# Graph transformer, then graph attention: scores and both contexts of a pair stand together in TensorE's order

## The chip, the core and the metric

The kernel runs on one core of one Trainium2 chip. The core has five engines that run side by side, each through its own instructions in order: TensorE (PE, matrix products), VectorE (DVE), ScalarE (ACT), GpSimd (POOL) and SyncE (SP, which here issues the DMAs). They wait for one another through semaphores. The metric is the time on the device in microseconds (us), lower is better. All arithmetic is float32.

## The reference

There are 128 graphs of 128 nodes with 512 features. Two layers follow one another, both ahead of them a layer norm and a relu, both with the input added at the end:

```python
h = relu(layernorm(x))
q, k, v = h @ Wq.T + bq, h @ Wk.T + bk, h @ Wv.T + bv      # 8 heads of 64
scores = (q @ k.T) / 8 * (adj + adj)                       # for each head, 128 x 128
attn = softmax(scores, axis=-1)
x = x + (attn @ v) @ Wo.T + bo                             # the contexts of all heads, side by side

h = relu(layernorm(x))
Wh = h @ W
e = leaky_relu(Wh @ a[:512] + (Wh @ a[512:]).T, 0.2)
att = softmax(where(adj > 0.5, e, -9e15), axis=1)
x = x + elu(att @ Wh)
```

## The kernel before

Graphs are handled in pairs (64 of them). The projections to q, k and v are made for two pairs at a time, by a scheme with seven products of half-size blocks instead of eight. The work is cut into some 130 small steps. A list, ORDER, says in which order the steps of different pairs are recorded: `name:lag` records step `name` of pair p - lag. Every engine runs its part of that list in order, so the list is the schedule.

The steps of the first layer's attention, for one graph `b` (graphs a and b of a pair are 2p and 2p + 1; step names in the margin are followed by a or b in the list):

```python
ps1 = ctx.enter_context(tc.tile_pool(name="ps1", bufs=6, space=PSUM))   # six banks for all other products
ps2 = ctx.enter_context(tc.tile_pool(name="ps2", bufs=1, space=PSUM))   # one score buffer, two banks
work = ctx.enter_context(tc.tile_pool(name="work", bufs=1))
...
def scores(b):                                     # sca, scb
    sc = ps2.tile([P, H, S], F32, name="sc", tag="ps2")
    for j in range(C):
        for s in range(2):
            r = slice(s * D, (s + 1) * D)          # 64 of the 128 rows of the array
            nc.tensor.matmul(sc[:, s * C + j, :], qT[r, j, cols], kT[r, j, cols], start=True, stop=True)

def weigh(b):                                      # ata, atb: scores times the adjacency
    at = work.tile([P, H, S], F32, name="at")
    nc.vector.scalar_tensor_tensor(at, scs.pop(b), QSCALE, adj..., op0=OP.mult, op1=OP.mult)

def maxima(b):                                     # mxa, mxb
    nc.vector.tensor_reduce(nmx, at, AX.X, OP.max, negate=True)

def exps(b, k):                                    # exa0 .. exa3: two heads each, on ScalarE
def shares(b, k):                                  # rca0, rca1: reciprocals of the sums
def normalise(b, k):                               # nma0 .. nma3: two heads each, on ScalarE

def flip_blocks(b):                                # fla, flb: 32 x 32 blocks transposed
    at = ats.pop(b)[0]
    trs[b] = work.tile([P, S // Q, H, Q], F32, name="tr")
    nc.vector.transpose(trs[b], at.rearrange("p h (j k) -> p j h k", k=Q))

def send_blocks(b):                                # bla, blb: to memory, one DMA
    nc.sync.dma_start(blocks[b]..., trs.pop(b)...)

def place_blocks(b):                               # pla, plb: back, each block to its place, four DMAs
    d = blocks.pop(b)
    aTs[b] = work.tile([P, S // Q, H, Q], F32, name="aT")
    for j in range(S // Q):
        nc.sync.dma_start(aTs[b][j * Q : (j + 1) * Q]..., d[:, :, j, :]...)

def context(b):                                    # pca, pcb
    aT = aTs.pop(b)
    pc = ps1.tile([P, C, S], F32, name="pc", tag="ps1")
    for j in range(C):
        for s in range(2):                         # 64 of the 128 columns of the array
            head = 2 * j + s
            nc.tensor.matmul(pc[s * D : (s + 1) * D, j, :], v[..., head * D : (head + 1) * D], aT[:, :, s * C + j, :],
                             start=True, stop=True)

def keep_context(b):                               # pea, peb
    nc.scalar.copy(rows_of(cxT, b % 2), pcs.pop(b))
...
for p in range(early, N + late):
    for step, lag in ORDER:
        pair = p - lag
        for do in tables.get(pair, {}).get(step), first_use.get((pair, step)):
            if do:
                do()
```

The other steps that are named later: U1 to U11 are the products for q, k and v of a later group, F the first evictions of their sums (ScalarE), A the additions (VectorE); o0 to o6 are the output products of the first layer and od their additions to x; st, pw, nm and h2 are the second layer norm, d the dot products with `a`, pb, wm, pr, m1, e1 and sw the second attention; g0, g1 gather with it, w0 to w6 are its products with W, zc and wd the evictions of those, ez, fa and fb the elu and the last additions, so the store. fa and fb are 1024-wide VectorE passes, as are hd0 and hd1 (the hidden rows of a later pair) and sh (a constant row).

Of the kernel before, what the change touches and what calls it, by code (L numbers as in the profile page):

```python
# [8 lines left out]
F32 = mybir.dt.float32  # L9
# [4 lines left out]
P = 128  # L14
# [3 lines left out]
H = 8  # L18
D = 64
Q = 32  # L20
# [4 lines left out]
def kernel(  # L25
# [19 lines left out]
    B, S, E = x.shape  # L45
# [9 lines left out]
    work = ctx.enter_context(tc.tile_pool(name="work", bufs=1))  # L55
# [5 lines left out]
    xs, x0s, adjs, adjTs, hAs, hSs = {}, {}, {}, {}, {}, {}  # L61
# [93 lines left out]
    def token_sum(h, s, k):  # L155

        if k == 0:
            nc.vector.tensor_tensor(s[:, 0], h[:, 2], h[:, 3], OP.add)
        elif k == 1:
            nc.vector.tensor_tensor(s[:, 1], s[:, 0], h[:, 0], OP.subtract)  # L160
        elif k == 2:
            nc.vector.tensor_tensor(s[:, 2], h[:, 0], h[:, 2], OP.subtract)
        else:
            nc.vector.tensor_tensor(h[:, 2], h[:, 1], s[:, 1], OP.subtract)
# [16 lines left out]
    st0, rows0, qks, vs, scs, ats, trs, blocks, aTs, pcs = ({} for _ in range(10))  # L181
# [45 lines left out]
            nc.vector.scalar_tensor_tensor(h, h, 0.0, row, op0=OP.max, op1=OP.mult)  # L227

    def hidden_sum(g, k):
        if k == 0:  # L230
            hSs[g] = grp.tile([P, 3, 2, 2 * S], F32, name="hS")
        token_sum(hAs[g], hSs[g], k)

# [119 lines left out]

    def flip_blocks(b):
        at = ats.pop(b)[0]
        trs[b] = work.tile([P, S // Q, H, Q], F32, name="tr")
        nc.vector.transpose(trs[b], at.rearrange("p h (j k) -> p j h k", k=Q))  # L357

    def send_blocks(b):
# [2 lines left out]

    def place_blocks(b):
        d = blocks.pop(b)
        aTs[b] = work.tile([P, S // Q, H, Q], F32, name="aT")
        for j in range(S // Q):
            nc.sync.dma_start(
                aTs[b][j * Q : (j + 1) * Q].rearrange("k i h q -> k i (h q)"), d[:, :, j, :].rearrange("i k x -> k i x")
            )
# [152 lines left out]
    def spread_u():  # L522
# [13 lines left out]
    ORDER = [  # L536
        (step.split(":")[0], int(step.split(":")[1]))
        for step in """
        w5:4 o4:2 ata:0 U2:0 w6:4 mxa:0 sw:3 pca:1 od4:2 plb:1 g0:3 zc5:4 o5:2 od4c:2 wd6:4 o6:2 fa:4 exa2:0 hs1:1
        g1:3 exa0:0 ez:4 F2:0 U1:0 ge0:3 U8:1 fb:4 exa1:0 ge1:3 od5:2 od6:2 rca0:0 exa3:0 st0:2 st1:2 gs0:3 t0:0  # L540
        rca1:0 w0:3 nma1:0 U4:0 w1:3 gs2:3 scb:0 pw:2 pcb:1 so:4 A3:20 nm:2 pea:1 t1:0 nma0:0 gs1:3 nma2:0 nma3:0
        gs3:3 zc0:3 h21:2 A8:1 A9:1 fla:0 U11:1 atb:0 h20:2 hs3:1 F4:0 mxb:0 peb:1 F1:0 U3:0 d10:2 o0:1 A11:1 F3:0
        d11:2 A7:-37 A2:0 U5:0 cs0:1 exb0:0 A10:28 f0:0 cs1:1 lT:0 lt:2 exb1:0 F5:0 exb2:0 A4:21 exb3:0 U6:0 rcb0:0
        nmb0:0 F6:0 wd1:3 U7:0 A5:0 F8:-10 F7:0 o1:1 F11:10 cs2:1 l0:-1 d00:2 hd0:0 rcb1:0 s0:0 A1:19 nmb1:0 w2:3
        hd1:0 nmb3:0 zc2:3 pb:2 U9:0 F9:0 hs0:0 lx:1 o3:1 A6:0 d01:2 w4:3 nmb2:0 wm:2 sh:1 bla:0 od0:1 la:-1 pr:2
        U10:0 w3:3 od1:1 o2:1 F10:0 hs2:0 pla:0 flb:0 m1:2 zc4:3 od2:1 sca:-1 blb:0 cs3:1 e1:2 wd4c:3
        """.split()
    ]

    def steps(p):  # L550
# [3 lines left out]
        for s, n in (("a", a), ("b", b)):  # L554
            table |= {
                "sc" + s: lambda n=n: scores(n),
                "at" + s: lambda n=n: weigh(n),
                "mx" + s: lambda n=n: maxima(n),
                "fl" + s: lambda n=n: flip_blocks(n),
                "bl" + s: lambda n=n: send_blocks(n),  # L560
                "pl" + s: lambda n=n: place_blocks(n),
                "pc" + s: lambda n=n: context(n),
                "pe" + s: lambda n=n: keep_context(n),
            }
            for k in range(4):
                table[f"ex{s}{k}"] = lambda n=n, k=k: exps(n, k)
                table[f"nm{s}{k}"] = lambda n=n, k=k: normalise(n, k)
            for k in range(2):
                table[f"rc{s}{k}"] = lambda n=n, k=k: shares(n, k)
# [41 lines left out]
        if odd and (g + 2) * 2 < N:  # L611
            for k in range(4):
                table[f"hs{k}"] = lambda k=k: hidden_sum(g + 2, k)
# [11 lines left out]
    with tc.manual_schedule():  # L625
# [10 lines left out]
        for k in range(4):  # L636
            hidden_sum(0, k)
        for n, u in enumerate(SEQ):
            firsts, adds = product(0, u[0], int(u[1]))
            if n == 2:  # L640
                weight_sums(wq_sb)
            if n == 4:
                first_stats(2)
            if n == 6:
                hidden_T(2, rows[2], "h2")
            if n == 8:
                weight_sums(wk_sb)
            if n == 10:
                first_stats(3)
            if n == 12:  # L650
                hidden_T(3, rows[3], "z")
                load_x0(4)
            if n == 14:
                for k in range(4):
                    hidden_sum(1, k)
            firsts()
            adds()
# [59 lines left out]
```

## Time and profile before

| | before |
|---|---|
| time, median of 3 runs | 2436.83 us (2435.96 to 2436.95) |
| span of the profiled run | 2433.9 us |
| granted TensorE clock, mean | 0.996 of full speed |
| TensorE matmul busy | 2395.6 us |
| VectorE busy | 1993.2 us |
| ScalarE busy | 1449.3 us |
| busiest kinds of matmul | seven-product projections (acc), output and second-layer products (row_a, row_c), scores (sc, 148.7 us), contexts (pc, 140.1 us) |

The profile is one execution on the chip. In it a float32 matmul stands as two records. A line of a group reads: source line, engine, operation, tile written <- tiles read, shapes, number, then busy time and mean ns of one, then the idle time of its engine just before, with what ended most of it. In a matmul's line `64*128` or `128*64` are the rows and columns of the array in use. In a timeline the records of one kind that follow one another are merged: start, time from the first start to the last end, number. The durations of matmuls overlap, so the time a group takes on TensorE is read from its start to the start of the next.

### The profile page before, as it was taken

The numbers are of one execution on the slowest core, as the hardware profiler recorded it, in microseconds if no ns is written. First come the engines' busy times: TensorE is split into PE (matmuls) and PEld (weight loads), VectorE is DVE, ScalarE is ACT, GpSimd is POOL, SyncE is SP. The second block draws the span as 40 slices with busy tenths as digits, with TensorE's granted clock in tenths as the row PEclk, the third lists the DMA queues.
The fourth block names the chain that finished last, engine by engine and source line by source line (L and its number), as shares of the span: only waits on it lengthen the run. The fifth ranks groups of instructions, "written<-read, shape, count | busy, mean of one in ns | idle before, by whom it ended". The sixth has DMA issues, their size and how long they took to land.

```text
span 2433.9 us, 40532 instructions
## 1 busy us (share of the span) xinstructions
PE 2395.6 (98%) x14264; PEld 2055.1 (84%) x14264; DVE 1993.2 (82%) x3909; ACT 1449.3 (60%) x4811; POOL 180.3 (7%) x323
## 2 busy tenths in 40 slices
PE   8999999999999999999999999999999999999987
PEld 7788888888888888888888888888888888888876
DVE  5788888888888888888888888888888888887786
ACT  2566556656565665565665656655656655666573
POOL 1000000000000000000000000000000000000000
PEclk9999999999999999999999999999999999999998
DMA  4435434445343454344453434453444544443331
GB/s 156 122 110 147 129 115 119 137 135 139 113 132 109 142 140 143 101 135 121 135 148 111 133 109 138 135 145 99 139 118 135 148 118 125 116 140 116 104 112 65
DMA packets 255275, 306.09 MB, mean 126 GB/s; under 512 B 21856, under 2 KB 181600, under 8 KB 254432
## 3 DMA queue, kind: packets, MB, share of 16 engines
q1 hardware_dynamic: 251568, 303.37, 42.7%
q8 instruction: 112, 1.84, 0.3%
q14 instruction: 91, 0.75, 0.1%
q0 software_dynamic: 1920, 0.13, 0.1%
q10 hardware_dynamic: 1584, 0.01, 0.0%
HBM read 202.64 MB, written 100.79 MB: 125 GB/s over the span
## 4 chain that ended last, share of the span: by engine, by line
PE 96%; DVE 2%; ACT 1%; issue 0%; DMA 0%; POOL 0%; SPq 0%; POOLq 0%; DVEq 0%; ACTq 0%
PE acc_a L261 27%; PE row_a L302 23%; PE acc_c L261 14%; PE row_c L302 9%; PE acc_b L261 7%; PE sc L323 6%; PE pc L386 5%; PE pg L464 5%; PE pb L432 1%; DVE junk L423 0%; DVE nmx L336 0%; PE pt L202 0%; ACT at L341 0%; DVE st L172 0%; DMA x<-in_x 0%
## 5 line engine op out<-in xcount | busy, mean ns | idle before, releaser
L341 ACT ACTIVATE at<-at,nmx 128x128 f32<-128x128 f32 x1024 | 398.6, 394 | 90.7 <-DVE nmx L336 90.6
L302 PE MATMUL row_a<-w,gT 128*128 128x256 f32 x1280 | 338.5, 388 | 15.1 <-DVE z L482 14.2
L350 ACT ACTIVATE at<-at,rs 128x128 f32<-128x128 f32 x1024 | 331.8, 394 | 0.0
L302 PE MATMUL row_a<-wo,cxT 128*128 128x256 f32 x1280 | 328.8, 380 | 0.1
L302 PEld LDWEIGHTS row_a<-w,gT 128*128 128x128 f32 x1280 | 239.3, 191 | 55.6 <-issue 9.2
L478 ACT COPY z<-row_a 128x256 f32<-128x256 f32 x256 | 94.9, 371 | 301.0 <-PE row_a L302 298.6
L302 PEld LDWEIGHTS row_a<-wo,cxT 128*128 128x128 f32 x1280 | 237.8, 190 | 30.8 <-DVE x L400 0.7
L400 DVE TENSOR_TENSOR x<-row_a,x 128x256 f32<-128x256 f32 x320 | 134.9, 422 | 144.5 <-PE row_a L302 139.8
L329 DVE SCALAR_TENSOR_TENSOR at<-sc,adj 128x1024 f32<-128x1024 f32 x128 | 156.8, 1225 | 98.5 <-PE sc L323 97.3
L278 ACT ACTIVATE kT<-acc_a,bk 128x256 f32<-128x256 f32 x256 | 107.5, 471 | 178.4 <-PE acc_a L261 178.4
L176 POOL TENSOR_SCALAR mv<-mv 128x2 f32<-128x2 f32 x128 | 32.8, 256 | 2196.3 <-ACT at L341 1858.8
L341 ACT ACTIVATION_READ_ACCUMULATOR at<-at,nmx 128x1 f32 x1024 | 195.3, 191 | 0.0
L278 ACT ACTIVATE qT<-acc_a,bq 128x256 f32<-128x256 f32 x256 | 105.7, 463 | 123.6 <-PE acc_a L261 123.6
L172 DVE BATCH_NORM_STATS2 st<-x 128x6 f32<-128x512 f32 x256 | 172.6, 674 | 4.7 <-DMA x<-in_x 4.6
L357 DVE STREAM_TRANSPOSE tr<-at 128x1024 f32<-128x1024 f32 x128 | 158.1, 1235 | 8.4 <-ACT at L350 8.3
L323 PEld LDWEIGHTS sc<-kT,qT 64*128 64x128 f32 x2048 | 124.2, 187 | 42.5 <-issue 42.1
L336 DVE TENSOR_REDUCE nmx<-at 128x8 f32<-128x1024 f32 x128 | 155.9, 1218 | 3.3
L323 PE MATMUL sc<-kT,qT 64*128 64x128 f32 x2048 | 148.7, 285 | 0.0
L464 PE MATMUL pg<-w,h 128*128 128x128 f32 x1024 | 141.2, 281 | 0.0
L464 PEld LDWEIGHTS pg<-w,h 128*128 128x128 f32 x1024 | 129.2, 191 | 14.0 <-issue 10.6
L386 PE MATMUL pc<-aT,v 128*64 128x128 f32 x2048 | 140.1, 279 | 0.0
L273 ACT COPY v<-acc_a 128x512 f32<-128x512 f32 x128 | 75.2, 587 | 104.2 <-PE acc_a L261 103.6
(126 smaller groups left out, 4925.4 us busy)
## 6 DMA issues: line engine op xcount, KB each, us to landing
blocks<-tr SPq DMA_DIRECT2D x128, 512.0 KB, 3.6
aT<-blocks SPq DMA_DIRECT2D x512, 128.0 KB, 2.9
x<-in_x SPq DMA_DIRECT2D x123, 512.0 KB, 6.6
out<-x SPq DMA_DIRECT2D x64, 512.0 KB, 3.8
hA<-in_xT SPq DMA_DIRECT2D x120, 256.0 KB, 4.6
mr<-rows SPq DMA_DIRECT2D x60, 256.0 KB, 4.7
adj<-in_adj SPq DMA_DIRECT2D x64, 128.0 KB, 5.2
adjT<-in_adjT SPq DMA_DIRECT2D x64, 128.0 KB, 4.3
```

What stands on the lines that cost most here:

```text
L172: nc.vector.bn_stats(st, src[:, i, :])
L261: nc.tensor.matmul(acc[:, m, :], lhsT, rhs, start=fresh and m == 0 and c == 0, stop=c == 1, skip_group_check=True)
L278: nc.scalar.activation(dst(t, f)[:, m, :], a[:, m, :], AF.Identity, bias=bias[:, j : j + 1])
L302: nc.tensor.matmul(acc, left[:, la, c, :], w[:, wb, c, :], start=n in (0, 3) and c == 0, stop=c == 1, skip_group_check=True)
L323: nc.tensor.matmul(sc[:, s * C + j, :], qT[r, j, cols], kT[r, j, cols], start=True, stop=True)
L329: nc.vector.scalar_tensor_tensor(at, scs.pop(b), QSCALE, adjs[p][:, i : i + 1, :].to_broadcast([P, H, S]), op0=OP.mult, op1=OP.mult)
L336: nc.vector.tensor_reduce(nmx, at, AX.X, OP.max, negate=True)
L341: nc.scalar.activation(at[:, j, :], at[:, j, :], AF.Exp, bias=nmx[:, j : j + 1], accum_out=sums[:, j : j + 1])
L350: nc.scalar.activation(at[:, j, :], at[:, j, :], AF.Copy, scale=rs[:, j : j + 1])
L357: nc.vector.transpose(trs[b], at.rearrange("p h (j k) -> p j h k", k=Q))
L386: nc.tensor.matmul(pc[s * D : (s + 1) * D, j, :], vs[b // G][:, b % G, head * D : (head + 1) * D], aT[:, :, s * C + j, :], start=True, sto ...
L464: nc.tensor.matmul(pg[:, c, :], h1s[p][0][:, i, c * P : (c + 1) * P], wts[p][:, i, :], start=True, stop=True)
```

## The change

In the list before, the scores of a, the context of a, and the scores and context of b stand at three places of a pair's iteration, with full-array matmuls between them. The new list brings them to one place: `sca:0 pca:1 pcb:1 scb:0`, that is scores of graph a, both contexts of the pair before, scores of graph b. The aim is that TensorE changes less often between its ways of dividing the array. Both transposed attentions of a pair must then be there at the same time. To have room for them, the flipped blocks and the transposed attention of a graph, which are not needed at once, share a buffer, one for graphs a and one for graphs b; before, there was one buffer for the flipped blocks and one for the transposed attention. The rest of the list was put in a new order around this.

```diff
@@ -227,7 +227,7 @@
             nc.vector.scalar_tensor_tensor(h, h, 0.0, row, op0=OP.max, op1=OP.mult)
 
     def hidden_sum(g, k):
-        if k == 0:
+        if g not in hSs:
             hSs[g] = grp.tile([P, 3, 2, 2 * S], F32, name="hS")
         token_sum(hAs[g], hSs[g], k)
 
@@ -353,7 +353,7 @@
 
     def flip_blocks(b):
         at = ats.pop(b)[0]
-        trs[b] = work.tile([P, S // Q, H, Q], F32, name="tr")
+        trs[b] = work.tile([P, S // Q, H, Q], F32, name="tr", tag=f"tr{b % 2}")
         nc.vector.transpose(trs[b], at.rearrange("p h (j k) -> p j h k", k=Q))
 
     def send_blocks(b):
@@ -362,7 +362,7 @@
 
     def place_blocks(b):
         d = blocks.pop(b)
-        aTs[b] = work.tile([P, S // Q, H, Q], F32, name="aT")
+        aTs[b] = work.tile([P, S // Q, H, Q], F32, name="aT", tag=f"tr{b % 2}")
         for j in range(S // Q):
             nc.sync.dma_start(
                 aTs[b][j * Q : (j + 1) * Q].rearrange("k i h q -> k i (h q)"), d[:, :, j, :].rearrange("i k x -> k i x")
@@ -536,14 +536,14 @@
     ORDER = [
         (step.split(":")[0], int(step.split(":")[1]))
         for step in """
-        w5:4 o4:2 ata:0 U2:0 w6:4 mxa:0 sw:3 pca:1 od4:2 plb:1 g0:3 zc5:4 o5:2 od4c:2 wd6:4 o6:2 fa:4 exa2:0 hs1:1
-        g1:3 exa0:0 ez:4 F2:0 U1:0 ge0:3 U8:1 fb:4 exa1:0 ge1:3 od5:2 od6:2 rca0:0 exa3:0 st0:2 st1:2 gs0:3 t0:0
-        rca1:0 w0:3 nma1:0 U4:0 w1:3 gs2:3 scb:0 pw:2 pcb:1 so:4 A3:20 nm:2 pea:1 t1:0 nma0:0 gs1:3 nma2:0 nma3:0
-        gs3:3 zc0:3 h21:2 A8:1 A9:1 fla:0 U11:1 atb:0 h20:2 hs3:1 F4:0 mxb:0 peb:1 F1:0 U3:0 d10:2 o0:1 A11:1 F3:0
-        d11:2 A7:-37 A2:0 U5:0 cs0:1 exb0:0 A10:28 f0:0 cs1:1 lT:0 lt:2 exb1:0 F5:0 exb2:0 A4:21 exb3:0 U6:0 rcb0:0
-        nmb0:0 F6:0 wd1:3 U7:0 A5:0 F8:-10 F7:0 o1:1 F11:10 cs2:1 l0:-1 d00:2 hd0:0 rcb1:0 s0:0 A1:19 nmb1:0 w2:3
-        hd1:0 nmb3:0 zc2:3 pb:2 U9:0 F9:0 hs0:0 lx:1 o3:1 A6:0 d01:2 w4:3 nmb2:0 wm:2 sh:1 bla:0 od0:1 la:-1 pr:2
-        U10:0 w3:3 od1:1 o2:1 F10:0 hs2:0 pla:0 flb:0 m1:2 zc4:3 od2:1 sca:-1 blb:0 cs3:1 e1:2 wd4c:3
+        F4:1 F6:1 flb:1 fb:4 U9:1 F9:1 g1:3 od5:2 ge1:3 o6:2 la:1 st0:2 s0:1 hd0:1 od6:2 U8:1 w0:3 st1:2 gs0:3 blb:1
+        hd1:1 pw:2 w1:3 gs1:3 nm:2 U10:1 zc0:3 so:4 U1:0 gs2:3 h20:2 A9:1 A8:1 l0:0 wd1:3 w2:3 F10:1 gs3:3 h21:2 plb:1
+        lx:1 hs0:1 zc2:3 lT:0 sca:0 pca:1 pcb:1 scb:0 w4:3 d00:2 d01:2 pea:1 A6:1 ata:0 mxa:0 peb:1 d10:2 w3:3 F1:0
+        d11:2 cs0:1 t1:0 exa1:0 f0:0 exa3:0 pb:2 sh:1 A4:4 wm:2 zc4:3 exa2:0 exa0:0 pr:2 o0:1 o1:1 rca1:0 F8:0 nma3:0
+        hs2:1 w5:3 hs1:1 wd4c:3 rca0:0 U2:0 nma1:0 cs2:1 cs1:1 nma2:0 m1:2 nma0:0 w6:3 od0:1 U11:1 od1:1 fla:0 U3:0
+        zc5:3 atb:0 F2:0 mxb:0 F3:0 o2:1 e1:2 A10:16 cs3:1 wd6:3 U5:0 F5:0 sw:2 exb0:0 A2:0 U4:0 exb2:0 A3:28 exb3:0
+        exb1:0 A5:0 A11:1 bla:0 o3:1 rcb1:0 od2:1 nmb2:0 U6:0 hs3:1 o4:1 lt:0 rcb0:0 nmb0:0 t0:0 nmb3:0 nmb1:0 pla:0
+        U7:0 ez:3 F7:0 F11:-22 g0:2 fa:3 od4:1 A1:15 od4c:1 ge0:2 o5:1 A7:14
         """.split()
     ]
```

## The prediction

> **What bounds the kernel now.** I read the table of engines first, then the busy time by stretches, then the chain that ended last.
>
> ```profile
> PE 2395.6 (98%) x14264; PEld 2055.1 (84%) x14264; DVE 1993.2 (82%) x3909; ACT 1449.3 (60%) x4811; POOL 180.3 (7%) x323
> ...
> PE 96%; DVE 2%; ACT 1%; issue 0%; DMA 0%; POOL 0%; SPq 0%; POOLq 0%; DVEq 0%; ACTq 0%
> ```
>
> ```profile
> 0.00:50.00 50.00, 39.93 (x187) 34.79 (x188) 28.34 (x52) 13.88 (x27) 4.79 (x15) 1.00 0.48 176
> 50.00:100.00 50.00, 44.59 (x260) 36.94 (x259) 38.13 (x69) 27.77 (x107) 5.25 (x9) 0.97 0.48 124
> ...
> 100.00:2300.00 2200.00, 2199.61 (x13173) 1891.51 (x13172) 1824.48 (x3570) 1334.17 (x4448) 165.25 (x289) 1.00 0.44 127
> ```
>
> The columns of the second view are the stretch, its length, then busy time of PE, PEld, DVE, ACT, POOL. From 100 to 2300 us TensorE is busy for 2199.6 of 2200 us, at full clock. There is nothing to hide behind it: the time falls only if TensorE's own queue gets shorter, and rises if TensorE starts to wait. But a busy TensorE need not be at its peak, so I looked at where each group of matmuls starts. This is TensorE's timeline in the middle of the kernel (start, duration of the merged group, instruction):
>
> ```profile
> 1211.12 1.03 PE L302 MATMUL row_c<-w,gT 128*128 128x256 f32 x4
> 1211.99 1.03 PE L302 MATMUL row_a<-wo,cxT 128*128 128x256 f32 x4
> 1212.94 1.16 PE L323 MATMUL sc<-kT,qT 64*128 64x128 f32 x16
> 1214.04 1.13 PE L302 MATMUL row_a<-w,gT 128*128 128x256 f32 x4
> 1215.00 1.03 PE L302 MATMUL row_a<-wo,cxT 128*128 128x256 f32 x4
> ...
> 1229.23 1.03 PE L302 MATMUL row_a<-w,gT 128*128 128x256 f32 x4
> 1230.19 1.16 PE L323 MATMUL sc<-kT,qT 64*128 64x128 f32 x16
> 1231.28 1.09 PE L386 MATMUL pc<-aT,v 128*64 128x128 f32 x16
> 1232.31 1.99 PE L261 MATMUL acc_c<-hA,wk 128*128 128x256 f32 x8
> 1234.14 1.89 PE L261 MATMUL acc_a<-wv,hS 128*128 128x256 f32 x8
> ```
>
> Durations overlap, so differences of starts are what counts. Four records of a full-array matmul normally take 0.87 us (1211.12 to 1211.99, or 216 ns a record). The four ahead of the scores take 0.95 (1211.99 to 1212.94), the four behind them 0.96 (1214.04 to 1215.00). Scores use half the rows of the array (64*128), contexts half the columns (128*64), everything else the whole. Record by record in the trace, the same numbers come back at every island of such matmuls: 93 ns extra on the last full-array step before one, 104 ns extra on the first step after one. Inside, score records run in pairs (one on each half of the array) 112 ns apart, so 8 pairs would take 0.90 us, but a group takes 1.092: about 95 ns are lost on its first pair and 97 on the way out. Context pairs are 109 ns apart, 0.872 for 8, and a group takes 1.024: 51 lost going in, 100 going out. A score group costs 1.092 and a context group 1.024 whether the neighbour is a full-array group or the other kind.
>
> [...] This trace agrees and gives the price: 0.197 us for leaving and re-entering full-array work, 0.196 us inside each score group, 0.152 us inside each context group. [...] busy time shows 100% while 0.2 us at a time goes into switching. [...] It matters for the one score buffer: emptying it takes VectorE 1225 ns a batch, longer than its score group.
>
> **The change part by part.** In the before order a pair of batches has three islands: scores of a alone, context of a alone, scores of b followed by context of b. In the after order it has one: scores a, context a, context b, scores b. The contexts belong to the pair before. I counted the switches in the two built programs' TensorE order: entries from full-array work fall from 193 to 65, context runs from 128 (of 8 matmuls) to 64 (of 16), score runs from 128 to 127 (the first pair has its two together).
>
> - 128 fewer islands x 0.1975 us = 25.3 us.
> - 64 context runs joined to another x 0.152 = 9.7 us.
> - 1 score run x 0.196 = 0.2 us.
>
> Together 35.2 us, or 0.55 us a pair, all of it on the path that sets the end. Nothing is added: no arithmetic of PE, DVE or ACT disappears or appears, and the DMAs are the same. The buffer change gives each batch parity one buffer that holds first the flipped blocks, then the transposed attention. That allows the two transposed attentions of a pair to be alive at once. The new test in the token sums only lets their steps come in another order. The other steps of the list are rotated and shuffled, none dropped. The shared buffer adds two waits: placing must follow the end of sending of the same batch (it did anyway, through memory), and the flip must follow the context of the pair before.
>
> Then the new order must not make TensorE wait. I walked one even and one odd pair by hand through the in-order queues, with times from the trace taken start to start: a 1024-wide VectorE pass 1.14 us (1.26 if the next reads it), a 512-wide add 0.60, a row add 0.34, statistics 0.80, an exponential with its sum 0.385, a scaling 0.292. These are the sizes and the waits that matter in the page:
>
> ```profile
> L329 DVE SCALAR_TENSOR_TENSOR at<-sc,adj 128x1024 f32<-128x1024 f32 x128 | 156.8, 1225 | 98.5 <-PE sc L323 97.3
> L357 DVE STREAM_TRANSPOSE tr<-at 128x1024 f32<-128x1024 f32 x128 | 158.1, 1235 | 8.4 <-ACT at L350 8.3
> L336 DVE TENSOR_REDUCE nmx<-at 128x8 f32<-128x1024 f32 x128 | 155.9, 1218 | 3.3
> ...
> blocks<-tr SPq DMA_DIRECT2D x128, 512.0 KB, 3.6
> aT<-blocks SPq DMA_DIRECT2D x512, 128.0 KB, 2.9
> ```
>
> Four places are close, timed from the start of a pair's iteration with TensorE never waiting:
>
> 1. Scores b need the one score buffer back. Scores a start at 11.33, their last record at 12.22. VectorE starts the masking 0.32 later in the trace, so at 12.54, and is done 1.26 later, at 13.80. Scores b are due at 11.33 + 1.09 + 1.02 + 0.87 = 14.31. Margin 0.5 us.
> 2. VectorE must be free at 12.54. Ahead of it lie the passes that wait for the last row product (3.66): row add and statistics to 4.9, the power on GpSimd to 6.3 while VectorE runs one wide pass to 6.35, then sums, adds and two dot products, 4.7 us more: 11.1. Margin 1.4 us.
> 3. The loop through the single attention buffer: mask, maxima, exponentials, scaling and flip of a, then of b. From 12.54 it gives the flip of a at about 23 and the flip of b at 33 (odd pair) to 35.6 (even pair, where an eviction of v holds ScalarE until 29.4); the iteration ends at 35.6 and 37.3. It closes.
> 4. Context b follows some 14 us after that flip of b: at worst the flip ends 0.5 us before its iteration does. Sending (3.6), four placings (1.75 to issue, 2.9 to land) make 7.8 in the next; context b is due at 13.4. Margin over 5 us.
>
> So the middle should run at 36.45 us a pair against 37.0. Start and end need their own estimate. At the start VectorE and ScalarE are slower than TensorE (constants are folded there: eight passes of 0.73, eight of 0.6), and TensorE sits idle 5.4 us between 50 and 100. The new order puts 177 - 169 = 8 fewer full matmuls of 0.43 us ahead of the first pair's second context, whose blocks arrive no earlier (about 91 us): some 3 us more idle, of which the first island's own wait, scores b right behind scores a, is part. At the end I walked the last two pairs: both contexts of the last pair now stand behind both placings, which leaves TensorE idle longer there, but the shift of the iteration shortens the rest. I get about as much idle time as before, within 5 us (before, TensorE is busy for 111.5 of the last 133.9 us by the same view of stretches: 22 idle).
>
> 2436.8 - 35.2 + 3 = 2404.6 us, which I round to 2404.5.
>
> **The rivals.**
>
> - The wait moves to scores b. If masking came 0.6 us later than I think, 64 pairs would lose 0.1 us each and little would be seen; at 1.1 us later the loss is 0.6 us a pair and the whole gain is gone (about 2440). For it: one score buffer, and VectorE is 82% busy. Against it: VectorE's idle time before the masking, 97.3 us over 62 waits, says that VectorE mostly waits for the scores here, not they for it.
> - Two contexts side by side still pay for their own changeover, for instance because the second has four DMA waits ahead of it. Then only the islands count: 2436.8 - 25.5 + 3 = 2414. Against it: inside a group the pairs alternate between column halves with no such cost.
> - The attention path becomes the bound: flip, send, place and context b form a loop with the shared buffer. If the DMA took twice its 6.5 us it would still fit; only a transfer held behind others on the one in-order issue queue could break it, at several us a pair (2450 and up). For it: the placing stands behind the store of another pair in that queue. Against it: that store is released by work done 1 us after the flip.
> - Start and end give more than the middle: a shorter pipeline could take 5 to 10 us off the end (2395 to 2400), a longer wait for the last contexts could add as much.
>
> **Range and chances.** The 35.2 us are counted from steps that repeat to the nanosecond, so the gain is sure unless a wait appears. The spread is start and end (5 us either way) and on the upper side a small wait in each pair: 2394 to 2422. A gain over 2% needs 48.7 us, 13.5 more than the switches hold, so I give it 0.05; a loss over 2% needs a new wait of 1.3 us in every pair, 0.03.
>
> **What would show it.** Right: an island whose groups start at 0, 1.09, 2.02 and 2.99 us, with full-array work again at 4.08; TensorE still busy without a break in the middle; 36.45 us a pair. Wrong in step 1 or 2: idle time of TensorE at the second scores, released by the masking. Wrong in the joined contexts: 16 context matmuls taking 2.05 instead of 1.90. Wrong in steps 3 and 4: idle time at a context, released by a DMA.

## The result, and the profile after

| | before | after |
|---|---|---|
| time, median (lowest to highest) | 2436.95 us (2435.96 to 2437.18) | 2413.79 us (2410.46 to 2416.30) |
| ratio | | 0.9904, 95% interval 0.9890 to 0.9918 |
| span of the profiled run | 2433.9 us | 2412.4 us |
| time at half TensorE clock in it | 17.1 us, in 3 spells | 30.7 us, in 7 spells |

The kernel is 1.0% faster. The time lies inside the predicted range and within 2% of before, as thought most likely; the middle value, 2404.5 us, was 9.3 us too low. The last row of the table is read from the clock records in the trace: each names a time from which TensorE runs at full or at half speed. Left out in both columns are a last spell, which begins behind the last matmul, and the start, up to the first clock record at 13.9 and 12.3 us, where matmuls run at half speed too (records of a transpose start 213 ns apart there in both kernels, 109 later; those of a projection 427 ns in the kernel before, 216 behind it). The prediction did not use these records.

The table of engines and the chain that ended last look as before:

```profile
PE 2366.6 (98%) x14264; PEld 2072.9 (86%) x14264; DVE 1993.3 (83%) x3909; ACT 1460.3 (61%) x4811; POOL 265.7 (11%) x323
...
PE 96%; DVE 2%; ACT 1%; DMA 1%; issue 0%; SPq 0%; POOL 0%; POOLq 0%; ACTq 0%; DVEq 0%
```

TensorE still bounds the kernel, with 29 us less of busy time and as many records. Busy time by stretches (stretch, length, busy time of PE, PEld, DVE, ACT, POOL, granted clock, share of DMA, GB/s):

```profile
50.00:100.00 50.00, 39.60 (x227) 32.95 (x226) 33.81 (x62) 22.36 (x84) 3.54 (x6) 0.90 0.36 101
100.00:2300.00 2200.00, 2199.93 (x13354) 1932.07 (x13353) 1849.98 (x3623) 1368.05 (x4529) 252.99 (x294) 1.00 0.47 128
```

Between 100 and 2300 us TensorE never waits, and gets through 181 records more than before in the same stretch. But in the 50 us ahead of it TensorE stands idle for 10.4 us instead of 5.4, and the granted clock is 0.90 instead of 0.97. TensorE's timeline at one island in the middle:

```profile
1213.29 1.03 PE L302 MATMUL row_a<-w,gT 128*128 128x256 f32 x4
1214.25 1.16 PE L323 MATMUL sc<-kT,qT 64*128 64x128 f32 x16
1215.34 1.97 PE L386 MATMUL pc<-aT,v 128*64 128x128 f32 x32
1217.24 1.16 PE L323 MATMUL sc<-kT,qT 64*128 64x128 f32 x16
1218.33 1.13 PE L302 MATMUL row_a<-w,gT 128*128 128x256 f32 x4
```

From scores a at 1214.25: contexts at 1.09, scores b at 2.99, full-array work at 4.08. The two contexts take 1.90 us together, so they share one way in and one way out. From the starts of the score groups between 150 and 2250 us, a pair takes 36.54 us on average, against 37.09 before: 0.546 us less. The waits of the whole run confirm that the island itself hardly ever waits:

```profile
L329 DVE SCALAR_TENSOR_TENSOR at<-sc,adj 128x1024 f32<-128x1024 f32 x128 | 156.7, 1225 | 94.8 <-PE sc L323 92.6
...
L323 PE MATMUL sc<-kT,qT 64*128 64x128 f32 x2048 | 150.3, 287 | 1.3 <-DVE at L329 1.3
...
L386 PE MATMUL pc<-aT,v 128*64 128x128 f32 x2048 | 128.4, 279 | 2.4 <-DMA aT<-blocks 2.4
```

VectorE still waits for the scores, and TensorE waits for the masking 1.3 us and for placed attention 2.4 us in all. Both waits belong to the first pairs. What TensorE does wait for stands at the start and at the end, where the number in brackets is idle time and its releaser:

```profile
78.44 3.78 PE L261 MATMUL acc_c<-wv,hA 128*128 128x256 f32 x8 [5.49 <-DVE v L282]
...
92.88 1.09 PE L386 MATMUL pc<-aT,v 128*64 128x128 f32 x16 [2.42 <-DMA aT<-blocks]
...
2320.97 1.03 PE L302 MATMUL row_c<-wo,cxT 128*128 128x256 f32 x4
2325.76 1.33 PE L302 MATMUL row_a<-wo,cxT 128*128 128x256 f32 x4 [3.77 <-DVE x L400]
2326.89 1.91 PE L464 MATMUL pg<-w,h 128*128 128x128 f32 x8
...
2355.34 2.08 PE L302 MATMUL row_a<-wo,cxT 128*128 128x256 f32 x4 [5.49 <-DVE x L400]
```

The second column shows a second loss behind the first. Eight records of a projection take 1.89 us elsewhere and 3.78 here; four of a row product take 1.03 us elsewhere and 2.08 here. Behind these waits TensorE runs at half speed: the granted clock is 0.50 from 80 to 84 us and from 2356 to 2360 us. Of the seven spells at half clock in the table, five last 3.413 us and two 6.827 us; of the three in the kernel before, one lasts 3.413 us and two 6.827 us.

So the middle did what was predicted, and the question is the 9 us in between. The theory: they lie at start and end, partly in longer waits, mostly in the slow clock behind the waits. The rivals: the prices of the switches were too high, or the margins in the island are smaller than worked out, so that the middle gives less than it could.

### The profile page after: what moved, and what is told of

Its sections match the earlier page's. It is cut to its first block, busy times and chain, and to the rows that moved or that the text cites. A ratio compares the mean times of both kernels' runs of the same rounds, so it can differ in the third digit from the quotient of the medians.

```text
span 2412.4 us, 40507 instructions
## 1 busy us (share of the span) xinstructions
PE 2366.6 (98%) x14264; PEld 2072.9 (86%) x14264; DVE 1993.3 (83%) x3909; ACT 1460.3 (61%) x4811; POOL 265.7 (11%) x323
## 4 chain that ended last, share of the span: by engine, by line
PE 96%; DVE 2%; ACT 1%; DMA 1%; issue 0%; SPq 0%; POOL 0%; POOLq 0%; ACTq 0%; DVEq 0%
PE acc_a L261 27%; PE row_a L302 23%; PE acc_c L261 13%; PE row_c L302 9%; PE acc_b L261 7%; PE sc L323 6%; PE pc L386 5%; PE pg L464 5%; PE pb L432 1%; ACT at L341 0%; ACT at L350 0%; PE pt L202 0%; DVE junk L517 0%; DVE tr L357 0%; DVE at L329 0%
## 5 line engine op out<-in xcount | busy, mean ns | idle before, releaser
L302 PE MATMUL row_a<-w,gT 128*128 128x256 f32 x1280 | 326.1, 385 | 7.7 <-DVE z L482 6.8
L302 PE MATMUL row_a<-wo,cxT 128*128 128x256 f32 x1280 | 322.3, 383 | 9.3 <-DVE x L400 9.3
L350 ACT ACTIVATE at<-at,rs 128x128 f32<-128x128 f32 x1024 | 316.5, 389 | 13.7 <-DVE rs L345 13.7
L176 POOL TENSOR_SCALAR mv<-mv 128x2 f32<-128x2 f32 x128 | 78.4, 613 | 2090.7 <-DVE mv L173 2090.7
L393 ACT COPY cxT<-pc 128x512 f32<-128x512 f32 x128 | 75.0, 586 | 136.5 <-PE pc L386 136.5
L464 PEld LDWEIGHTS pg<-w,h 128*128 128x128 f32 x1024 | 136.2, 194 | 8.6 <-ACT w L452 1.8
L177 POOL TENSOR_TENSOR mv<-mv,mhalf 128x2 f32<-128x2 f32 x128 | 140.6, 1099 | 10.7
```

The lines of the kernel that those rows point to most:

```text
L177: nc.gpsimd.tensor_tensor(mv[:, :, 1], mv[:, :, 1], mhalf.to_broadcast([P, 2]), OP.pow)
L302: nc.tensor.matmul(acc, left[:, la, c, :], w[:, wb, c, :], start=n in (0, 3) and c == 0, stop=c == 1, skip_group_check=True)
L350: nc.scalar.activation(at[:, j, :], at[:, j, :], AF.Copy, scale=rs[:, j : j + 1])
L464: nc.tensor.matmul(pg[:, c, :], h1s[p][0][:, i, c * P : (c + 1) * P], wts[p][:, i, :], start=True, stop=True)
```

## The experiments

Each was also compared with the kernel before on the same chip (2435.6 to 2436.1 us).

### Contexts apart: scores b right behind the first context

```diff
-        sca:0 pca:1 pcb:1 scb:0 w4:3
+        sca:0 pca:1 scb:0 pcb:1 w4:3
```

> The changed kernel, with the island in the order scores a, context a, scores b, context b. Theory (each change of the way the array is divided has its own price, and the one score buffer leaves 0.5 us of margin): two context groups of 1.02 us instead of one of 1.90, so 0.15 us a pair more; and scores b would be due 2.11 us after the start of scores a, while masking hands the buffer back after about 2.47, so TensorE waits some 0.4 us in every pair. Together 0.5 us a pair, 63 pairs: 2413.8 + 33 = 2447 us, and the start of scores b is seen 2.5 us after that of scores a. Rival (contexts pay nothing for standing apart, only islands count): the wait alone, 2439.

Measured: 2445.45 us (one run). The timeline:

```profile
1228.21 1.16 PE L323 MATMUL sc<-kT,qT 64*128 64x128 f32 x16
1229.31 1.09 PE L386 MATMUL pc<-aT,v 128*64 128x128 f32 x16
1230.70 1.16 PE L323 MATMUL sc<-kT,qT 64*128 64x128 f32 x16 [0.30 <-DVE at L329]
1231.79 1.09 PE L386 MATMUL pc<-aT,v 128*64 128x128 f32 x16
```

TensorE is held up until the score buffer comes back, 2.49 us after scores a start. In the changed kernel scores b are due at 2.99. The margin of step 1 is 0.50 us, as predicted. A pair takes 37.07 us, 0.525 more than in the changed kernel: 0.15 for the switches of a second context run, and 0.37 by which scores b come late (2.49 us instead of the 2.12 that scores and one context take), of which the trace shows 0.30 as idle time. So the order inside the island matters: with the contexts apart, a pair takes as long as before (37.09), and the whole kernel is 9 us slower than before. Those 9 us must lie at start and end.

### Two islands again: one full-array product between the contexts and scores b

```diff
-        sca:0 pca:1 pcb:1 scb:0 w4:3
+        sca:0 pca:1 pcb:1 w4:3 scb:0
```

> The changed kernel, with one full-array product of the second layer between the contexts and scores b, so that a pair has two islands again and its contexts still stand together. Theory: one more leaving and re-entering of full-array work, 0.1975 us a pair, 63 pairs: 12.4 us, 2426 us, with no wait. Rival (the joined contexts alone carry the gain): no change, 2414.

Measured: 2427.10 us (one run). A pair takes 36.740 us against 36.542: 0.198 us for one island more, the price that the prediction took from the kernel before (0.1975). The prices were not too high.

### The buffers alone

The list of before, with the two shared buffers of after:

```diff
-        trs[b] = work.tile([P, S // Q, H, Q], F32, name="tr")
+        trs[b] = work.tile([P, S // Q, H, Q], F32, name="tr", tag=f"tr{b % 2}")
-        aTs[b] = work.tile([P, S // Q, H, Q], F32, name="aT")
+        aTs[b] = work.tile([P, S // Q, H, Q], F32, name="aT", tag=f"tr{b % 2}")
```

> The kernel before, its own list, with only the shared buffer of flipped blocks and transposed attention for each batch parity. Theory: the buffer only makes room and costs no time by itself: 2437 us within 1. Rival (the new waits between flip, sending and placing cost or save something in every pair): a difference of 6 us or more (0.1 us a pair).

Measured: 2436.12 us, before on this chip 2436.06. By themselves the buffers neither give nor take.

### The new order without the shared buffers

One buffer for flipped blocks and one for transposed attention, as before. The second placing must then stand between the contexts; two loads stand behind it:

```diff
-        ... h21:2 plb:1 lx:1 hs0:1 zc2:3 lT:0 sca:0 pca:1 pcb:1 scb:0 w4:3
+        ... h21:2 hs0:1 zc2:3 sca:0 pca:1 plb:1 lx:1 lT:0 pcb:1 scb:0 w4:3
```

> The changed kernel without its second part: one buffer for flipped blocks and one for transposed attention, as before, instead of one per batch of the pair that serves as both. The placing of the second attention must then wait until the first context has read the buffer, so it stands between the two contexts, with two loads moved behind it. Theory: sending is long done, but four placings take 1.75 us to issue and 2.9 to land, and the second context waits for them inside the island: 4 to 5 us a pair, after which TensorE runs 3.4 us at half clock, 1.7 us lost: 5.5 to 7 us a pair, 2750 to 2860. Rival: only the wait counts and the full clock holds: 2660 to 2720. If the shared buffer were not needed for the joined contexts: under 2440.

Measured: 2838.14 us (one run). TensorE's timeline, and in the groups the row of the contexts:

```profile
1207.89 1.09 PE L386 MATMUL pc<-aT,v 128*64 128x128 f32 x16
1213.64 1.74 PE L386 MATMUL pc<-aT,v 128*64 128x128 f32 x16 [4.65 <-DMA aT<-blocks]
```

```profile
L386 PE MATMUL pc<-aT,v 128*64 128x128 f32 x2048 | 190.0, 344 | 288.7 <-DMA aT<-blocks 288.7
```

The second context waits some 4.5 us in every pair (288.7 us in all, 2.4 in the changed kernel), and 341 us run at half clock, in 68 spells (mean granted clock 0.939). At half clock the eight records of a projection took 3.78 us instead of 1.89, so half of the time in which TensorE works at it is put down as lost: by the clock records and TensorE's busy time 294.9 us here and 28.0 in the changed kernel, which makes 133 us. With 286 us more of these waits the sum is 420, against 424 measured. So the shared buffers bring no time themselves, but without them the new order is far slower than the old. It is also the attention path as the bound, the third rival of the prediction, made real, and dearer than its wait because of the clock.

### Kept warm: spare matmuls in the waits

The changed kernel, with full-array matmuls whose results nobody reads put ahead of its long waits, into the score buffer while that is free. They are extra work of 18.6 us:

```diff
+        def warm(n):
+            t = ps2.tile([P, H, S], F32, name="warm", tag="ps2")
+            for _ in range(n):
+                nc.tensor.matmul(t[:, 0:2, :], ident, wq_sb[:, 0, 0, :], start=True, stop=True)
+        fill = {(0, "U9"): 11, (61, "o4"): 8, (60, "w2"): 4, (62, "o4"): 9, (61, "w2"): 4, (62, "w2"): 4, (63, "g0"): 3}
...
+                if (pair, step) in fill:
+                    warm(fill[pair, step])
```

> The changed kernel, with spare full-array matmuls into the free score buffer where TensorE waits at start and end: 11 ahead of the wait at 73 us, 8 and 9 ahead of the third-quarter output products of the last pairs but two and but one, 3 or 4 at four shorter waits, 18.6 us of work in all and none of it needed. Theory (what start and end took beyond the estimate is the halved clock that follows a wait, 30.7 us at half speed in the profile against 17.1 before): the clock stays up, and 5 to 10 us come back, 2404 to 2409 us, though more work is done. Rival (the waits themselves are the loss, the slow clock falls beside them): no change or some us longer, 2413 to 2418.

Measured: 2408.00 us (2407.52 to 2408.50), ratio to before 0.9884 (0.9867 to 0.9900): 5.8 us below the changed kernel (4.9 by the two ratios), by doing more. The end:

```profile
2320.96 1.03 PE L302 MATMUL row_c<-wo,cxT 128*128 128x256 f32 x4
2321.82 3.62 PE L672 MATMUL warm<-wq,ident 128*128 128x256 f32 x16
2325.76 1.13 PE L302 MATMUL row_a<-wo,cxT 128*128 128x256 f32 x4 [0.32 <-DVE x L400]
2326.72 1.05 PE L464 MATMUL pg<-w,h 128*128 128x128 f32 x8
```

The row product behind the wait starts at 2325.76 in both kernels: the wait for VectorE is no shorter. What follows is: the gathering product takes 1.05 us instead of 1.91. One spell of 6.8 us at half clock is left, behind a wait of 4.1 us at the start. Over the whole run TensorE is busy with its useful matmuls for 10.7 us less than in the changed kernel (2355.9 against 2366.6 us), but idle time and spare matmuls together take 50.3 us where idle time took 45.9: part of what the faster clock saves turns into longer waits.

### Constants folded later

The constants of the output product were folded on VectorE ahead of work of the first pair that TensorE waits for. Here they stand behind the flip of its second graph:

```diff
-            (0, "mxa"): constant_c, (0, "mxb"): lambda: weight_sums(wo_sb), (0, "atb"): constant_u,
+            (0, "mxa"): constant_c, (0, "flb"): lambda: (weight_sums(wo_sb), constant_u()),
```

> The changed kernel, with the folding of the two row constants and the sums of the output weight (8.3 us of VectorE) moved from the first masking and maxima of graph b of the first pair to behind the flip of that graph, where VectorE waits for scores anyway. Theory (start loses 5.7 us because TensorE waits for an addition that stands behind those constants on VectorE): that wait goes, the blocks of the first pair arrive some 6 us earlier, but TensorE arrives earlier too and then waits about 5 us for them: half to three quarters of 6 us come back, 2408 to 2411. Rival (the wait is set by the softmax of the first pair on ScalarE, the constants fall beside it): 2413 to 2415.

Measured: 2409.07 us (2408.88 to 2411.67), ratio 0.9891 (0.9877 to 0.9906). That is 4.7 us below the changed kernel (3.2 by the two ratios to before), so a part of the miss lies at the start. In the trace the wait of 5.49 us at 78 us is gone; one of 4.57 us for the second context of the first pair stands in its place, where the changed kernel waits 2.42. Half clock takes 30.7 us in this run too, so this gain is not one of the clock.

```profile
87.73 1.97 PE L386 MATMUL pc<-aT,v 128*64 128x128 f32 x16 [4.57 <-DMA aT<-blocks]
```

### Another order at the start, at the end, and both

At the start, with the constants later, three projections stand ahead of the first contexts (and two evictions ahead of keeping them). At the end, the last pair's scores a and its softmax stand at the front of its iteration:

```diff
+        orders[1] = moved(moved(ORDER, "U2:0 U3:0 U5:0", ahead="sca:0"), "F2:0 F3:0", ahead="pea:1")
```
```diff
+        last = moved(ORDER, "sca:0", ahead="F4:1")
+        last = moved(last, "ata:0 mxa:0", behind="flb:1")
+        last = moved(last, "exa1:0 exa3:0 exa2:0 exa0:0", behind="ge1:3")
+        last = moved(last, "rca1:0 rca0:0 nma3:0 nma1:0 nma2:0 nma0:0", behind="st1:2")
+        orders[N - 1] = [x for x in last if x != ("la", 1)]
+        orders[N - 2] = moved(ORDER, "la:0", behind="lT:0")
```

> As the run with the constants later, and three products of the second pair's iteration (5.2 us of TensorE work that is due later in it anyway) stand ahead of its first scores. Theory (at the start TensorE only waits, at both places, for work that takes its time elsewhere; filling the waits with useful products removes waits and the slow clock behind them): start loses some 10 us less than in the changed kernel, 2403 to 2406. Rival (the wait only moves on to the next pair's context, for every later step is pushed back too): no better than the constants alone.

> The changed kernel, but in the last pair's own iteration the scores of its graph a, their masking, softmax and scaling stand at the front, so that they no longer wait behind the second layer's products of an earlier pair; its adjacency is loaded one iteration sooner. Theory (at the end TensorE is idle because the last pair's attention chain starts late: its scores stand behind a product that waits for statistics, about 8 us): 5 to 9 us come back, 2405 to 2409. Rival (the end is bound by the number of steps on VectorE, not by their order): within 2 us of 2413.8.

> Both: constants later, three products ahead at the start, and the last pair's scores ahead at the end. Theory: start and end do not touch each other, so the gains add up: 2395 to 2401. Rival (the run is bound by one of the two only): as the better of the two alone.

Measured, in this order: 2410.22 us (2407.96 to 2412.64, ratio 0.9894, 0.9879 to 0.9908), 2417.99 (2415.13 to 2419.92, 0.9924, 0.9910 to 0.9939) and 2414.87 (2411.56 to 2415.43, 0.9910, 0.9893 to 0.9926). All three theories missed; of the rivals, that of the start order came true. The start order gives nothing beyond the later constants, the end order costs some 4 us, with times that just overlap, and both together are no better than the changed kernel. The start order shows why:

```profile
88.16 1.97 PE L386 MATMUL pc<-aT,v 128*64 128x128 f32 x32 [1.34 <-DVE v L282]
90.06 1.16 PE L323 MATMUL sc<-kT,qT 64*128 64x128 f32 x16
91.15 1.99 PE L302 MATMUL row_a<-wo,cxT 128*128 128x256 f32 x8
97.53 2.08 PE L302 MATMUL row_a<-wo,cxT 128*128 128x256 f32 x4 [4.38 <-DVE x L400]
```

The wait of 4.57 us for placed blocks is gone, with 1.34 us for an addition in its place, and 4.38 us stand a few groups further on, ahead of an output product, again with the half clock behind them. At the end it is the same:

```profile
2341.25 2.08 PE L302 MATMUL row_a<-w,gT 128*128 128x256 f32 x4 [5.82 <-DVE z L482]
```

This wait was 1.93 us in the changed kernel; the next one fell from 5.49 to 4.16. The waits that VectorE releases were moved by reordering, not removed. Whether the amount of VectorE's work or the chain of its steps holds them in place, no run here shows.

### Constants later and warm, and the same for the kernel before

The two edits that helped, together; the fill at the start now stands ahead of the first pair's second context, in the buffer which that context then overwrites:

```diff
         pc = ps1.tile([P, C, S], F32, name="pc", tag="ps1")
+        for _ in range(36 if b == 1 else 0):
+            nc.tensor.matmul(pc[0:D, 0, :], ident[:, 0:D], wq_sb[:, 0, 0, 0:S], start=True, stop=True)
```

> The changed kernel with the constants folded later and, in the waits of its start and end, spare matmuls whose results nobody reads: 36 half-width ones ahead of the second context of the first pair (3.9 us, into the buffer that this context then overwrites), and full-array ones in the waits of the last pairs as in the run that kept TensorE warm. Theory: [...] Constants later alone gave 2409.1, warm alone 2408.0; what is left at half clock in the first is some 24 us at the end and 7 us at the start, so both together give 2401 to 2405, with under 7 us at half clock. Rival: the two gains are the same gain (the start is bound by VectorE and ScalarE whatever TensorE's clock): 2407 to 2409.

Measured: 2404.40 us (2404.01 to 2404.82), ratio 0.9870 (0.9854 to 0.9885). It is below each of the two edits alone (2408.00 and 2409.07), so the two gains are not one. Behind the start there is no half clock until the last matmul. The views by stretches of the changed kernel and of this one, for the same stretch of the end:

```profile
2330.00:2360.00 30.00, 22.58 (x139) 19.22 (x138) 23.49 (x49) 18.50 (x65) 1.09 (x2) 0.84 0.35 110
```

```profile
2330.00:2360.00 30.00, 25.71 (x168) 21.43 (x167) 24.86 (x54) 19.58 (x67) 1.91 (x3) 1.00 0.43 130
```

The clock is 1.00 instead of 0.84. Two figures of the expectation were wrong. All 36 spare matmuls stand on the same half of the columns, and their 72 records take 7.7 us, not 3.9. And with the constants later alone, half clock took 20.5 us at the end and 10.2 at the start, not 24 and 7.

The control is the kernel before, warmed. In a first form the spare matmuls stood one step behind its wait at 70 us and one pair behind those at the end:

```diff
+        fill = {(0, "U9"): 10, (61, "w2"): 10, (62, "w2"): 3, (63, "w2"): 9}
```

> A control: the kernel before, with spare full-array matmuls in its four long waits (10 at 70 us, 10, 3 and 9 at the end), nothing else changed. It has 17 us at half clock in three spells, so at most 8.5 us to win against 31 us and 15 in the changed kernel. Theory: the change made the slow clock dearer; before kept warm gains 3 to 6 us (2430 to 2433), and about as much as the changed kernel gains by the same means (5.8) or less. Rival: spare matmuls help both kernels for another reason than the clock: before gains 8 us or more (2428 or less).

Measured: 2444.27 us (2443.52 to 2445.54), ratio 1.0033 (1.0020 to 1.0045): 8 us slower.

```profile
74.94 3.65 PE L261 MATMUL acc_a<-wv,hA 128*128 128x256 f32 x8 [4.75 <-ACT v L273]
78.43 4.48 PE L672 MATMUL warm<-wq,ident 128*128 128x256 f32 x20
```

The wait is as long as ever, with the half clock behind it, and then 4.48 us of matmuls come on top. Over the run 13.7 us at half clock are left. In the second form they stand ahead of the waits:

```diff
-        fill = {(0, "U9"): 10, (61, "w2"): 10, (62, "w2"): 3, (63, "w2"): 9}
+        fill = {(0, "U7"): 10, (60, "w2"): 10, (61, "w2"): 3, (62, "w2"): 9}
```

> The control again, with the spare matmuls where the waits are: 10 (4.3 us) ahead of the wait at 70 us, and 10, 3 and 9 (4.3, 1.3 and 3.9 us) ahead of the three waits at 2365, 2390 and 2404 us; in the run before they stood one step behind the first and one pair behind the others. Theory: the kernel before has 17 us at half clock against 31 of the changed one, so at most 8.5 us to win; spare matmuls win 3 to 7 us (2429 to 2433), and the changed kernel with the constants later, warmed in the same way (2404.4), is then 25 to 29 us ahead, near the middle's share of 33.5 less what longer waits at start and end take. Rival: the waits of before, fewer and apart, cost it no clock worth having: 2435 or more.

Measured: 2431.26 us (2430.15 to 2432.52), ratio 0.9981 (0.9973 to 0.9989).

```profile
69.52 4.48 PE L672 MATMUL warm<-wq,ident 128*128 128x256 f32 x20
74.41 1.99 PE L261 MATMUL acc_a<-wv,hA 128*128 128x256 f32 x8 [0.41 <-ACT v L273]
```

Half clock falls from 17.1 to 3.4 us and the time by 4.6. The same matmuls help inside a wait and hurt behind it, so it is not their mere presence that helps. But the slow clock costs the kernel before too, and filling its waits is worth nearly as much there as in the changed kernel (5.8, or 4.9 by the ratios). With both warmed, at 2431.26 and 2408.00 us, the change is worth 23.3 us, as it is without (23.2). With the constants later besides, the changed kernel is 26.9 us ahead, within the 25 to 29 expected; what later constants would do for the kernel before was not run.

## Why the prediction was right and where it was not

**What bounds the kernel, and the sum of the switches: right.** 0.546 us less a pair, times 64, is 34.9 us, against 35.2 predicted. The pair itself takes 36.54 us, not 36.45, because it took 37.09 before, not 37.0. The price of an island was seen a second time by putting one back (0.198 us). Contexts that only change the column half join without a price: two take 1.90 us, the 1.02 of one and 0.87 more. Scores next to contexts pay: a score group takes 1.09 us there too, where its 8 pairs of records, 112 ns apart, would take 0.90.

**Step 1, the score buffer: right to the figure.** Margin 0.50 us against 0.5, measured by taking it away.

**Steps 2, 3 and 4: no wait in the middle shows any of them wrong.** VectorE still waits for scores, and DMA releases a context late only in the first pairs. That the sharing of buffers is what keeps step 4 wide was shown by the run without it.

**The rivals.** Contexts side by side pay no changeover (1.90 us, not 2.05). The wait did not move to scores b, and the attention path did not become the bound. The fourth rival had the right place, start and end, and one of its two signs.

**Start and end: this is the step that failed.** It read "some 3 us more idle" for the start and "about as much idle time as before, within 5 us" for the end, and priced nothing else. For the profiled runs, whose spans differ by 21.5 us where the prediction's terms give 32.2:

| | predicted | measured |
|---|---|---|
| switches | -35.2 | -34.9 |
| idle time of TensorE, 0 to 100 us | +3 | +4.7 (20.2 against 15.5) |
| idle time from 2300 us to the end | 0 | +3.1 (25.5 against 22.4) |
| half clock, at half its time | none | +6.8 ((30.7 - 17.1) / 2) |
| sum | -32.2 | -20.3 (spans: -21.5) |

Counting only the time in which TensorE works at half clock gives nearly the same last term (28.0 us against 14.1, half of the difference is 6.9), so that does not explain the 1.2 us by which the sum misses the spans. Two small terms that the table lacks do: idle time in the middle (0.1 us against 0.4), and the half speed ahead of the first clock record, which delays the kernel before by 0.7 us more (its first group of eight projection records takes 2.58 us, 1.91 in the changed kernel). The two estimates of idle time were 1.7 and 3.1 us short, the second inside its own margin of 5. The larger part is a term that was not in the sum. A wait of TensorE was priced at its length, but the matmuls behind it take up to half of a spell at half clock longer besides (spells of 3.4 and 6.8 us in these two traces; 1.89 us more for the eight projection records above). The prediction noted "at full clock" for the middle and did not ask what the clock does in the two stretches where it expected waits, though the view it showed had 0.97 there.

That start and end cost more than 3 us is seen three times: with 64 times the gain of a pair taken off, the change loses 11.8 us there, and the single runs with the contexts apart and with two islands lose 10.8 and 13.3. That the slow clock costs time is shown too: with the waits filled, 5 to 6 us came back, though no wait on VectorE became shorter. Not shown is that it alone made the miss: warmed, the kernel before gained nearly as much, and the change is worth 23 us either way. Half clock and waits are not independent, since a part of what TensorE saves is spent in the next wait (10.7 us saved, 4.4 of it spent, in the run kept warm). So the table says where the time lies, not what each term would bring back.

That the time still lies in the range is partly luck. Start and end were given 3 us, 5 either way, and took 11.8; the upper edge of 2422 stood there for a small wait in each pair, which did not come.

The start was also argued with the wrong instruction. The wait was expected at the second context; the longest one was for the addition of v, held up behind the constants (5.49 us), and the one at the context was 2.42.

The times of one kernel spread with the clock. Of 41 runs of the kernel before that accompanied the experiments, those with a mean granted clock of 0.996 took 2434.5 to 2436.7 us, those with 0.994 took 2437.1 to 2438.2. The changed kernel's spread (2410.5 to 2416.3) narrows to 1 us in its two warmed versions; the kernel before, warmed and at 0.999 in all of its 14 runs, still spreads by 2.4. That the clock's spells fall differently from run to run fits this; the last section has one wait that had a spell behind it in one trace and none in two.

What stays open is the rest of the waits at start and end. They are released by VectorE, and no version here makes that work shorter. Of the three moves, later constants gained 3 to 5 us; the two other orders only moved the waits.

## What to carry to other kernels

When TensorE is the bound and busy all the time, count how often it changes between its ways of dividing the array, take the price of a change from differences of starts, and then join equal pieces as far as buffers allow; look for the buffer that the joining needs, since it may be worth nothing by itself and everything to the order. Price a wait of TensorE at its length and up to half of the slow spell behind it (3.4 or 6.8 us long in the two traces here), less what the next wait would have taken anyway, and when a change shortens the middle by making start and end emptier, read the granted clock there too. Ahead of waits that couldn't be removed, spare matmuls paid here, in both kernels; a step too late they were pure cost. And give the kernel before the same treatment before saying how much of the gap it closes.

## What the runs showed of the hardware

- How short a wait had half clock behind it. From 40 us on to the last matmul, the profiled runs of the kernel before and of the changed one have 11 waits of TensorE of 1.93 us or more. At 10 of them a spell at half clock begins near the end of the wait (from 1.9 us before it to 1.8 us after it); the shortest three of these, 1.93 us each at the end of the changed kernel, have spells of 3.4 us. The one without is 2.20 us long and ends at 2345.7 us in the kernel before. None of the 8 waits of 0.9 to 1.5 us has a spell.
- The same wait in three traces. It takes 2.20 us in the kernel before, 2.19 in its first warmed form and 2.20 in the second. The first two have no spell there (granted clock 1.00 from 2330 to 2360 us; the four records behind the wait take 1.10 us in the first warmed form). The second warmed form has one (granted clock 0.91 from 2330 to 2350 us, 1.51 us for the four records). So the length of the wait alone doesn't tell whether half clock follows.
- Where the spells begin. In each of the two profiled runs, before and changed, the starts of all spells lie whole multiples of the shortest spell's length (3.413 us) apart, to 3 ns. With the time from 40 us on to the last matmul cut into stretches of that length at these starts, a stretch at full clock with 1.93 us or more of idle TensorE was followed by half clock in 10 of 10 cases, one with 1.0 to 1.74 us in none of 9. In the kernel before, such a cut divides the wait of 2.20 us into 1.74 and 0.45. That these counts hold beyond the two traces was not shown.
- The 16 records of a context, whose matmuls alternate between the halves of the columns, take 0.87 us without what is lost going in and out (kernel before); the 72 spare records on one half (changed kernel, constants later and warm) took 7.7 us, 107 ns each instead of 54. Those also write one place again and again, which no run here separates from the half.
